# Four product buffers instead of six, delta*x for all channels at once, and an earlier bound for parts on TensorE

## The chip, the cores and the metric

The kernel runs on one core of one Trainium2 chip. The metric is the device time of one execution in microseconds (us). Three timed runs of the kernel before gave 22,543.33, 22,549.62 and 22,551.03 us; the median is 22,549.62 us. The engines are called PE (TensorE, matmul), DVE (VectorE), ACT (ScalarE), POOL (GpSimd) and SP (SyncE, which issues most DMAs).

## The reference

The input is a batch of 8 images of 56 x 56 pixels with 192 channels. Four layers follow one another, each of the form x = x + f(groupnorm(x)): a gated Toeplitz mixer, a shifted-window attention, a depthwise 3 x 3 convolution, and a selective scan in four directions. The change lies in the last. Its core, with 384 inner channels, 16 states and L = 3,136 pixels, is:

```
delta = softplus(delta + delta_bias)
dA    = exp(delta * A)                  # per channel, state, pixel
dBu   = (delta * u) * B                 # u is the convolved input
hs    = scan(a1*a2, a2*b1 + b2)         # h[t] = dA[t]*h[t-1] + dBu[t]
y     = sum over states of hs * C  + D * u
```

The four directions are added up, then come a layer norm over channels, a gate and an output projection.

## The kernel before, in words

Two early stages (the mixer's projections and its Toeplitz products) run alone, up to about 2,340 us, and the front (below) of the first image after them. From 3,735 us on everything is organised around one long loop over the scan.

**Pairs.** The scan's work is cut into chunks of 448 pixels: 8 images (`b`), 4 directions (`slot`) and 7 chunks (`j`), 224 chunks in all. A chunk has 3 blocks of 128 channels (`d`) and 8 groups of two states (`k`). One (chunk, `d`, `k`) is a pair, and a batch is the 672 pairs of one image; there are 5,376 pairs. For pair number `g` the kernel issues:

- `inject` (L990): POOL multiplies du = delta*x by B into `hs` (five buffers);
- `decay` (L1000): ACT computes exp(delta*A) into a PSUM tile `ps_a` (two buffers), two instructions;
- `initial` and `keep_state`: ACT copies the state in and out;
- `scan` (L1010): DVE scans, 898 elements a partition;
- `times_c` (L1019): the product h*C into `hc` (six buffers), on POOL for k in 1, 4, 6 and on DVE for the other five;
- `add_up` (L1032): PE adds the two halves of `hc` into `ps_y`, by two matmuls with the identity.

`times_x` (L979) computes du for one channel block on POOL, from `delta` and a tile `xcd` that `load_xc` (L968) brings in; both have two buffers. `load_xc` also serves the sums of slot 2, through `xds`: it is issued at k = 2 and read at k = 4. `load_bc` brings B and C for the next chunk while the last channel block runs, and `load_delta` brings delta for the next chunk at (d, k) = (1, 0).

**Parts.** Beside the pairs run the parts. `front(b)` holds all other layers of the next image: gate, attention, conv2, inner (input projection and convolution) and steps (delta, B and C of the scan). `finish` holds the norm, the gate and the output projection of eight rows of a finished image. Both are generators; at each `yield` the planner may go on to the next piece. `front` works in one SBUF area (`slab`), so one image's front follows the other. The convolution of inner is issued in thirds of three matmuls (L803) and then evicted by ACT (L812). A front must have stored a chunk's delta before its scan may begin; the loop forces the front at (1, 0) of the chunk before, where that isn't so (L1176).

**The order.** All is written out by hand in one static order for each engine, by the loop at L1168. In iteration `g` it issues, in this order: the du work if it is due, `inject` of g+2, the product of g-1 if it is POOL's, `keep_state` of g-1, `decay` of g+1, `initial` of g+2, `scan` of g, the product of g if it is DVE's, loads, the sums of a finished channel block, then pieces of parts (`parts.step`), and `add_up` of g-2. The planner (`Parts`, L1053) keeps a booked time for P, A, D and E (POOL, ACT, DVE, PE), with costs written in the code: 2.09 us for an inject, 1.1 us on E for an `add_up`, 0.60 us for a matmul of 448 columns. `n1` is the booked begin of the next scan. A piece of a part goes in if its booked ends stay inside the limits of L1221; each refusal adds 3.0 us of grace (L1074). A part that holds a PSUM bank after a piece waits for the next step (L1099).

The program does not take waits from this booking: engines wait for each other by the real dependences and buffers alone.

Of the kernel before, what the change touches and what calls it, by code (L numbers as in the profile page):

```python
# [15 lines left out]
F32 = mybir.dt.float32  # L16
# [11 lines left out]
CH = 448  # L28
# [5 lines left out]
ND = DI // 128  # L34
NG = 2
# [46 lines left out]
def model(ctx: ExitStack, tc: tile.TileContext, a: dict, out: bass.AP):  # L82
# [144 lines left out]
    with (  # L227
# [9 lines left out]
        for ax in range(2):  # L237
# [4 lines left out]
            for c0 in range(D1 // CP):  # L242
# [8 lines left out]
                for c1 in range(0, CP, TC):  # L251
                    t = tm[n_t % 3]
                    n_t += 1
                    e = ext[1 - ax][c0 * CP + c1 : c0 * CP + c1 + TC, :]
# [25 lines left out]
    with (  # L280
# [54 lines left out]
        for i in range(WS):  # L335
            for u in range(2):
                for j in range(WS):
                    at = (i * 2 + u) * WS + j
# [614 lines left out]
        bms, cms, deltas, dus, xcs, states, hss, das, hcs, yps, xds = ({} for _ in range(11))  # L953
# [6 lines left out]
        def load_bc(i, k):  # L960
            b, slot, j = chunks[i]
            for ts, name, r0 in ((bms, "bm", 0), (cms, "cm", NS)):
                ts[i, k] = bcp.tile([128, NG, CH], F32, name=name)
                r = slot % 2 * 32 + r0 + NG * k
                src = bc_d[slot // 2][b][r : r + NG, j * CH : (j + 1) * CH]
                nc.sync.dma_start(out=ts[i, k], in_=src.unsqueeze(0).to_broadcast([128, NG, CH]))

        def load_xc(i, d):  # L968
            b, slot, j = chunks[i]
            t = sp.tile([128, CH], F32, name="xcd", bufs=2)  # L970
            nc.sync.dma_start(out=t, in_=xc_d[slot // 2][b][:, d, j * CH : (j + 1) * CH])
            return t

        def load_delta(i):
            b, slot, j = chunks[i]
            delta = deltas[i] = delta2[:, i % 2]
            nc.sync.dma_start(out=delta[:, :, 1 : CH + 1], in_=dl_d[slot][b][:, :, j * CH : (j + 1) * CH])

        def times_x(i, d):  # L979
            du = dus[i, d] = sp.tile([128, 1, CH], F32, name="du", bufs=2)  # L980
            nc.gpsimd.tensor_mul(du[:, 0, :], deltas[i][:, d, 1 : CH + 1], xcs.pop((i, d)))  # L981

        def tokens(i):

            return (slice(0, CH), CH, 0) if chunks[i][1] % 2 else (slice(1, CH + 1), 0, CH)

        def on_pool(d, k):
            return k in (1, 4, 6)

        def inject(g):  # L990
            i, d, k = pairs[g]
            hs = hss[g] = sp.tile([128, NG, CH + 1], F32, name="hs", bufs=5)
            nc.gpsimd.tensor_mul(hs[:, :, tokens(i)[0]], dus[i, d].to_broadcast([128, NG, CH]), bms[i, k])  # L993

        def initial(g):
            i, d, k = pairs[g]
            src = zero2 if i % NCH == 0 else states[i - 1][:, d, NG * k : NG * k + NG]
            nc.scalar.copy(hss[g][:, :, tokens(i)[1]], src)  # L998

        def decay(g):  # L1000
            i, d, k = pairs[g]
            slot = chunks[i][1]
            dA = psa.tile([128, 1024], F32, name="ps_a")
            dA = das[g] = dA[:, : NG * (CH + 1)].rearrange("p (n t) -> p n t", n=NG)
            at = slot % 2
            for n in range(NG):
                c = NG * k + n
                nc.scalar.activation(  # L1008
                    dA[:, n, :], deltas[i][:, d, at : at + CH + 1], AF.Exp, scale=negA[:, slot, d, c : c + 1]
                )  # L1010
# [8 lines left out]
        def times_c(g):  # L1019
            i, d, k = pairs[g]  # L1020
            h = hss[g] if on_pool(d, k) else das[g]
            hc = hcs[g] = sp.tile([128, NG, CH], F32, name="hc", bufs=6)
            (nc.gpsimd if on_pool(d, k) else nc.vector).tensor_mul(hc, h[:, :, tokens(i)[0]], cms[i, k])  # L1023

        def keep_state(g):
# [27 lines left out]
        class Parts:  # L1053
# [8 lines left out]
            def run(self, engine, cost, *after):  # L1062
                self.t[engine] = max(self.t[engine], 0.0, *after) + cost
                return self.t[engine]
# [72 lines left out]
        with tc.manual_schedule():  # L1137
            for k in range(NP):
                load_bc(0, k)
            load_delta(0)  # L1140
            xcs[0, 0] = load_xc(0, 0)
            times_x(0, 0)
            ahead, last = 2, len(pairs) - 1
            parts = Parts()
            run = parts.run

            fed, set_, scanned, taken, summed = ([0.0] * (len(pairs) + ahead + 8) for _ in range(5))

            def feed(g):
                inject(g)  # L1150
                fed[g] = run("P", 2.09, taken[g - 5] if g > 4 else 0.0)

            def take(g):
                times_c(g)
                after = scanned[g], summed[g - 6] if g > 5 else 0.0
                taken[g] = run("P", 2.0, *after) if on_pool(*pairs[g][1:]) else run("D", 1.09, *after)

            def prepare(g):
                decay(g)
                set_[g] = run("A", 1.3, taken[g - 2] if not on_pool(*pairs[g - 2][1:]) else scanned[g - 2])  # L1160

            for g in range(ahead):
                feed(g)
            initial(0), initial(1)
            prepare(0)
            ahead_of, b_next = None, 1
            ending, anything = None, dict.fromkeys("ADE", 1e9)
            for g, (i, d, k) in enumerate(pairs):  # L1168
                b, slot, j = chunks[i]
                if ahead_of not in parts.clients and b_next < B:  # L1170
                    ahead_of = parts.add(front(b_next), "front")
                    b_next += 1
                more = i + 1 < len(chunks)
                if more and d == 1 and k == 0:
                    b1, slot1, j1 = chunks[i + 1]
                    while (b1, slot1 // 2, j1) not in made:  # L1176
                        parts.step(anything, ahead_of)
                    load_delta(i + 1)
                if k in (0, 3) and (d + 1 < ND or more):
                    at = (i, d + 1) if d + 1 < ND else (i + 1, 0)  # L1180
                    if k == 0:
                        xcs[at] = load_xc(*at)
                    else:
                        times_x(*at)
                        run("P", 1.08)
                pi, pd, pk = pairs[g - 1]
                if g + ahead <= last:
                    feed(g + ahead)
                if g and on_pool(pd, pk):
                    take(g - 1)  # L1190
                if g:
                    keep_state(g - 1)
                    run("A", 0.15, scanned[g - 1])
                if g < last:
                    prepare(g + 1)
                if g + 2 <= last:
                    initial(g + 2)
                    run("A", 0.12, taken[g - 3] if g > 2 else 0.0)
                scan(g)
                scanned[g] = run("D", 2.02, set_[g], fed[g])  # L1200
                if not on_pool(d, k):
                    take(g)
                if g and pd == ND - 1 and pi + 1 < len(chunks):
                    load_bc(pi + 1, pk)
                done = (i, d - 1) if d else (i - 1, ND - 1)
                if k == 2 and g > NP and chunks[done[0]][1] == 2:
                    xds[done] = load_xc(*done)
                if i % (4 * NCH) == 0 and b > 0 and (d, k) == (1, 4):
                    while ending.at < 3:
                        parts.step(anything, ending)  # L1210
                if k == 4 and g > NP:
                    sums(*done)
                pb, pslot, pj = chunks[i - 1]
                if i and pslot == 1 and (d, k) == (0, 5):
                    while ending in parts.clients:
                        parts.step(anything, ending)
                    ending = parts.add(finish(pb, pj), "finish")

                n1 = max(parts.t["D"], fed[g + 1], set_[g + 1])
                n2 = n1 + (2.02 if on_pool(*pairs[min(g + 1, last)][1:]) else 3.11)  # L1220
                parts.step({"A": max(n2, fed[g + 2]) - 0.7, "E": n1 + 8.0, "D": 0.2})  # L1221
                if g >= 2:
                    add_up(g - 2)
                    summed[g - 2] = run("E", 1.1, taken[g - 2])
            if on_pool(d, k):
                times_c(last)
            for g in (last - 1, last):
                add_up(g)
            while parts.clients:
                parts.step(anything)  # L1230
            sums(i, d)
            drain(finish(b, j))
# [101 lines left out]
```

## Time and profile before

| what | value |
|---|---|
| median of 3 runs | 22,549.62 us |
| profiled execution: its own time | 22,537.83 us |
| its span | 22,536.1 us |
| PE busy | 18,327.5 us (81%) |
| DVE busy | 16,594.4 us (74%) |
| POOL busy | 16,169.7 us (72%) |
| ACT busy | 12,468.3 us (55%) |
| first and last scan of the loop | 3,735 us, 22,497 us |
| mean granted TensorE clock | 0.90 |
| DMA over the span | 143 GB/s |

The busy times are of one profiled execution. A busy PE is an upper bound, since matmuls are pipelined and the end of each is modelled: the records of `add_up` have a mean of 593 ns but follow each other every 375 ns where they are back to back. Line numbers (L993 and so on) are those of the kernel before. In the lists of waits, "A <- B" says that the engine and line A stood idle and that B's instruction released it. Of one batch, that of the sixth image's front, the stages lie at 15,808 (gate), 16,323 (attention), 17,099 (conv2), 17,338 (inner) and 17,861 to 18,145 us (steps).

### The profile page before, as it was taken

What the parts mean: (1) busy time and instruction counts of PE and PEld (TensorE: products, weight loads), DVE (VectorE), ACT (ScalarE), POOL (GpSimd) and SP (SyncE); (2) the same over time, 40 slices, a digit from 0 to 9 for tenths busy, and PEclk for the clock granted to TensorE, in tenths of its full rate; (3) what the DMA queues carried; (4) which work ended last, traced back from release to release, by engine and by line L of the source; (5) the groups of instructions that cost most, each with busy time, mean ns of one, the idle gap of its engine ahead of it and who ended that gap; (6) DMA issues with size and microseconds to landing.
All of it is one profiled execution on the core that took longest, in us unless ns stands there. A gap on an engine that the chain in (4) does not pass through costs nothing. (4 is left out here: it accounts for less than half of the span.)

```text
span 22536.1 us, 200417 instructions
## 1 busy us (share of the span) xinstructions
PE 18327.5 (81%) x58660; PEld 9644.0 (43%) x58660; DVE 16594.4 (74%) x13156; ACT 12468.3 (55%) x31864; POOL 16169.7 (72%) x8500
## 2 busy tenths in 40 slices
PE   8866677878888889888887888788978897887666
PEld 4566433434443344434443444344533443343233
DVE  3211113997799868997899779976998789968998
ACT  3311234664757566655766566747675666556555
POOL 0000003897889778887898778977897789878999
PEclk9988777999999989999999989998999999998888
DMA  3478215444554455444644455345544554444443
GB/s 90 106 197 189 73 48 159 139 132 143 187 149 123 136 170 167 126 124 159 195 133 124 151 185 146 123 144 182 158 129 131 174 178 124 131 157 165 130 129 114
DMA packets 2536334, 3220.40 MB, mean 143 GB/s; under 512 B 1045261, under 2 KB 2488687, under 8 KB 2504272
## 3 DMA queue, kind: packets, MB, share of 16 engines
q1 hardware_dynamic: 2515010, 3091.32, 46.3%
q0 software_dynamic: 15520, 116.14, 1.4%
q8 instruction: 465, 7.62, 0.1%
q14 instruction: 635, 5.20, 0.1%
q10 hardware_dynamic: 4704, 0.12, 0.0%
HBM read 2631.56 MB, written 575.48 MB: 142 GB/s over the span
## 5 line engine op out<-in xcount | busy, mean ns | idle before, releaser
L993 POOL TENSOR_TENSOR hs<-du,bm 128x896 f32<-128x896 f32 x5376 | 11132.9, 2111 | 53.7 <-DVE ps_a L1017 35.3
L1038 PE MATMUL ps_y<-hc,ident_sb 128*128 128x448 f32 x21504 | 9850.6, 593 | 717.1 <-POOL hc L1023 624.2
L1017 DVE TENSOR_TENSOR_SCAN ps_a<-ps_a,hs 128x898 f32<-128x898 f32 x3360 | 6800.2, 2024 | 1630.8 <-ACT ps_a L1008 1365.3
L1008 ACT ACTIVATE ps_a<-delta,A_logs_sb 128x449 f32<-128x449 f32 x10752 | 6860.9, 638 | 543.6 <-DVE hs L1017 273.4
L1038 PEld LDWEIGHTS ps_y<-hc,ident_sb 128*128 128x128 f32 x21504 | 4296.7, 208 | 4800.2 <-issue 3550.5
L1023 POOL TENSOR_TENSOR hc<-hs,cm 128x896 f32<-128x896 f32 x2016 | 4086.4, 2027 | 1966.0 <-DVE hs L1017 1236.0
L1017 DVE TENSOR_TENSOR_SCAN hs<-ps_a,hs 128x898 f32<-128x898 f32 x2016 | 4065.2, 2016 | 481.1 <-ACT ps_a L1008 337.5
L1023 DVE TENSOR_TENSOR hc<-ps_a,cm 128x896 f32<-128x896 f32 x3360 | 3668.6, 1092 | 278.0 <-PE ps_y L1038 47.5
L1030 ACT COPY state<-ps_a 128x2 f32<-128x2 f32 x3359 | 527.9, 157 | 3604.9 <-DVE hc L1023 3601.7
L981 POOL TENSOR_TENSOR du<-delta,xcd 128x448 f32<-128x448 f32 x672 | 723.7, 1077 | 1397.5 <-DMA xcd<-xc 1384.5
L263 PE MATMUL ps_tz<-tzx,tm 112*112 112x112 f32 x4608 | 889.2, 369 | 466.0 <-issue 298.0
L803 PE MATMUL ps_f<-slab 128*128 128x448 f32 x2646 | 1105.1, 554 | 102.0 <-DMA slab<-dg_d 78.7
L277 POOL DMA_DIRECT2D o<-tzx x192 | 98.0, 514 | 1493.2 <-DVE tzx L269 1017.3
L263 PEld LDWEIGHTS ps_tz<-tzx,tm 112*112 112x112 f32 x4608 | 883.7, 199 | 471.8 <-issue 470.6
L269 DVE COPY tzx<-ps_tz 112x448 f32<-112x448 f32 x288 | 180.0, 625 | 1174.6 <-PE ps_tz L263 800.9
L76 PE MATMUL ps_f<-slab 96*96 96x448 f32 (+6 forms) x2306 | 746.1, 519 | 88.9 <-DMA slab<-x 37.2
L633 PE MATMUL ps_f<-ident_sb,slab 98*98 98x98 f32 x1344 | 334.6, 316 | 594.6 <-ACT slab L626 594.6
L269 ACT COPY tzx<-ps_tz 112x448 f32<-112x448 f32 x288 | 153.3, 532 | 1200.5 <-PE ps_tz L263 982.3
L998 ACT COPY hs<-state 128x2 f32<-128x2 f32 x4608 | 817.4, 177 | 0.0
L803 PEld LDWEIGHTS ps_f<-slab 128*128 128x128 f32 x2646 | 512.9, 195 | 603.3 <-issue 533.3
L735 PE MATMUL ps_f<-slab 96*96 96x448 f32 x1764 | 732.4, 551 | 41.7 <-DVE slab L722 41.2
L618 ACT ACTIVATE slab<-slab,mxs 98x98 f32<-98x98 f32 x1344 | 489.4, 365 | 359.7 <-DVE mxs L615 359.7
(215 smaller groups left out, 17601.5 us busy)
## 6 DMA issues: line engine op xcount, KB each, us to landing
bm<-bc SPq DMA_DIRECT2D x1792, 448.0 KB
cm<-bc SPq DMA_DIRECT2D x1792, 448.0 KB
xcd<-xc SPq DMA_DIRECT2D x840, 224.0 KB
dl<-slab SPq DMA_DIRECT2D x224, 672.0 KB
delta<-dl SPq DMA_DIRECT2D x224, 672.0 KB
tzx<-qv SPq DMA_DIRECT2D x192, 588.0 KB
o<-tzx POOLq DMA_DIRECT2D x192, 588.0 KB, 16.7
slab<-x SPq DMA_DIRECT2D x224, 336.0 KB
```

Source lines behind the costliest of these rows:

```text
L76: return f(*args, **kw)
L263: nc.tensor.matmul(po[:, c, :], t[:, c2 + c, :], x[:, :, c1 + c2 + c], start=True, stop=True)
L735: nc.tensor.matmul(p[:CP, :CH], dg[:, k, t, :], xp[:, u, k, dy : dy + 8, dx : dx + W], start=t == 0, stop=t == 8,)
L803: nc.tensor.matmul(p[:, :CH], dg[:, t, :], xp[:, 8 * j + dy : 8 * j + dy + 8, dx : dx + W], start=t == 0, stop=t == 8,)
L981: nc.gpsimd.tensor_mul(du[:, 0, :], deltas[i][:, d, 1 : CH + 1], xcs.pop((i, d)))
L993: nc.gpsimd.tensor_mul(hs[:, :, tokens(i)[0]], dus[i, d].to_broadcast([128, NG, CH]), bms[i, k])
L998: nc.scalar.copy(hss[g][:, :, tokens(i)[1]], src)
L1008: nc.scalar.activation(dA[:, n, :], deltas[i][:, d, at : at + CH + 1], AF.Exp, scale=negA[:, slot, d, c : c + 1])
L1017: nc.vector.tensor_tensor_scan(h, dA, hs, 0.0, ALU.mult, ALU.add)
L1023: (nc.gpsimd if on_pool(d, k) else nc.vector).tensor_mul(hc, h[:, :, tokens(i)[0]], cms[i, k])
L1030: nc.scalar.copy(states[i][:, d, NG * k : NG * k + NG], h[:, :, tokens(i)[2]])
L1038: nc.tensor.matmul(yps[i, d][:, :CH], ident, hcs[g][:, n, :], start=k + n == 0, stop=k + n == NP + NG - 2)
```

## The change

Three edits go together.

1. `hc` has four buffers instead of six. The planner's `take` books a product behind the sum of pair g-4 instead of g-6.
2. `xcd` and `du` have four buffers instead of two. The three `load_xc` of the next chunk are issued together, at (d, k) = (1, 0) right behind `load_delta`, and the three `times_x` of the next chunk at (1, 6), (1, 7) and (2, 0). Before, each was loaded at k = 0 and multiplied at k = 3 of the channel block before. The first chunk gets all three ahead of the loop.
3. A part's booked end on E has to lie at most 5.0 us behind `n1`, instead of 8.0 us.

The buffers given and taken have the same size in sum: two `hc` of 3,584 bytes a partition, against two `xcd` and two `du` of 1,792 bytes each.

```diff
         def load_xc(i, d):
-            t = sp.tile([128, CH], F32, name="xcd", bufs=2)
+            t = sp.tile([128, CH], F32, name="xcd", bufs=4)
...
         def times_x(i, d):
-            du = dus[i, d] = sp.tile([128, 1, CH], F32, name="du", bufs=2)
+            du = dus[i, d] = sp.tile([128, 1, CH], F32, name="du", bufs=4)
...
         def times_c(g):
-            hc = hcs[g] = sp.tile([128, NG, CH], F32, name="hc", bufs=6)
+            hc = hcs[g] = sp.tile([128, NG, CH], F32, name="hc", bufs=4)
...
             load_delta(0)
-            xcs[0, 0] = load_xc(0, 0)
-            times_x(0, 0)
+            for d in range(ND):
+                xcs[0, d] = load_xc(0, d)
+                times_x(0, d)
...
             def take(g):
                 times_c(g)
-                after = scanned[g], summed[g - 6] if g > 5 else 0.0
+                after = scanned[g], summed[g - 4] if g > 3 else 0.0
...
                     load_delta(i + 1)
-                if k in (0, 3) and (d + 1 < ND or more):
-                    at = (i, d + 1) if d + 1 < ND else (i + 1, 0)
-                    if k == 0:
-                        xcs[at] = load_xc(*at)
-                    else:
-                        times_x(*at)
-                        run("P", 1.08)
+                    for e in range(ND):
+                        xcs[i + 1, e] = load_xc(i + 1, e)
+                if more and (d, k) in ((1, 6), (1, 7), (2, 0)):
+                    times_x(i + 1, d + k - 7 if d == 1 else 2)
+                    run("P", 1.08)
...
-                parts.step({"A": max(n2, fed[g + 2]) - 0.7, "E": n1 + 8.0, "D": 0.2})
+                parts.step({"A": max(n2, fed[g + 2]) - 0.7, "E": n1 + 5.0, "D": 0.2})
```

## The prediction

> **What bounds the kernel now.** I read the groups of instructions first, for what one pair costs each engine; then busy time by stage; then the waits of the worst stage. From the groups (busy time, mean ns | idle ahead of them):
>
> ```profile
> L993 POOL TENSOR_TENSOR hs<-du,bm 128x896 f32<-128x896 f32 x5376 | 11132.9, 2111 | 53.7 <-DVE ps_a L1017 35.3
> L1038 PE MATMUL ps_y<-hc,ident_sb 128*128 128x448 f32 x21504 | 9850.6, 593 | 717.1 <-POOL hc L1023 624.2
> L1023 POOL TENSOR_TENSOR hc<-hs,cm 128x896 f32<-128x896 f32 x2016 | 4086.4, 2027 | 1966.0 <-DVE hs L1017 1236.0
> L1023 DVE TENSOR_TENSOR hc<-ps_a,cm 128x896 f32<-128x896 f32 x3360 | 3668.6, 1092 | 278.0 <-PE ps_y L1038 47.5
> L981 POOL TENSOR_TENSOR du<-delta,xcd 128x448 f32<-128x448 f32 x672 | 723.7, 1077 | 1397.5 <-DMA xcd<-xc 1384.5
> ```
>
> Per pair POOL needs 2.09 (its usual duration) + 3/8 x 2.03 + 1/8 x 1.08 = 2.99 us, DVE 2.02 + 5/8 x 1.09 + about 0.1 = 2.8 us. The loop's 5,376 scans run from 3,735 to 22,497 us, 3.49 us a pair; the last batch, with no front beside it, takes 3.0. So 0.5 us a pair comes from the parts. Three stretches (attention, inner, last batch; columns as in the head line):
>
> ```profile
> core 0: us, PE busy (x) PEld busy (x) DVE busy (x) ACT busy (x) POOL busy (x), PEclk, DMA share, GB/s
> 16323.00:17031.00 708.00, 565.19 (x2027) 276.29 (x2028) 672.68 (x565) 499.09 (x1574) 660.59 (x339) 0.93 0.40 123
> 17338.00:17805.00 467.00, 413.40 (x1099) 213.45 (x1100) 330.00 (x218) 247.35 (x576) 360.89 (x188) 0.93 0.47 150
> 20600.00:22000.00 1400.00, 949.72 (x1937) 423.25 (x1936) 1320.60 (x848) 738.67 (x1936) 1400.00 (x727) 0.86 0.40 128
> ```
>
> The last stretch is POOL's, 100%. Attention runs DVE and POOL at 95% and 93%, 3.15 us a pair. In inner they fall to 71% and 77% and a pair takes 3.9 to 4.5 us: TensorE binds there. Four records of a sum take 1.5 us at their spacing of 0.375 us, a convolution third of six takes 2.25, together 3.75 us. The waits from 17,350 to 17,800 us (total, times, longest):
>
> ```profile
> ACT slab L812 <- PE ps_f L803: 103.1, 18, 9.5
> ...
> DVE ps_a L1017 <- ACT ps_a L1008: 64.3, 28, 5.3
> POOL hc L1023 <- DVE hs L1017: 45.7, 14, 7.9
> ...
> DVE hs L1017 <- ACT ps_a L1008: 20.8, 9, 4.6
> ```
>
> ACT stands at the eviction of a convolution, the decays behind it are late, then DVE, then POOL. One such moment in order of time:
>
> ```profile
> 17526.39 1.09 DVE L1023 TENSOR_TENSOR hc<-ps_a,cm 128x896 f32<-128x896 f32 x1 [0.73 <-PE ps_y L1038]
> ...
> 17528.65 0.63 ACT L812 ACTIVATE slab<-ps_f,cb_sb 128x448 f32<-128x448 f32 x1 [7.64 <-PE ps_f L803]
> ...
> 17533.88 2.02 DVE L1017 TENSOR_TENSOR_SCAN hs<-ps_a,hs 128x898 f32<-128x898 f32 x1
> ...
> 17536.04 2.08 POOL L1023 TENSOR_TENSOR hc<-hs,cm 128x896 f32<-128x896 f32 x1 [7.50 <-DVE hs L1017]
> ```
>
> The first line is a product waiting 0.73 us for a buffer although there are six.
>
> **What the Trainium skill says.** "TensorE: Matmul & The Clock Gate", Architectural detail: ACT and DVE are strict FIFO, and matmuls keep program order. The lines above agree: decays stand 7.64 us behind one eviction. "FP8 and Floating Point Precision", TensorE Precision Notes: true FP32 takes four passes; here each 448-column matmul of the source is two records, 0.75 us together, while the planner books 0.55 to 0.60. "Perfetto Trace Analysis", Optimization Strategy: a gap that repeats can mean too few buffers for the next tile; with six, products waited for sums 190.7 us (47.5 on DVE, 143.2 on POOL). "SBUF — State Buffer", SBUF: two separate sides: the DVE/GpSimd port lock needs a DVE operation with two SBUF inputs. Scan and product on DVE have one input in PSUM, so moving du should start no new contention; inject's usual 2.09 us is the same in both middle stages.
>
> **The change, part by part.**
>
> *hc from six to four.* A product of pair g now needs the sum of g-4 finished. Behind a waiting DVE product stand the next scan, then ACT's decay of g+2 (two ps_a buffers); behind a POOL product stand inject and the finish part's multiplies L915 and L922; SP's reload of cm waits too. I laid every product's start in the trace against the end of the sum four pairs back: 641 DVE products would have waited 1,557 us and 193 POOL products 442 us, nearly all in the stages of conv2 to steps. That 1,999 us is the upper bound. If instead the idle time that DVE has ahead of its scans swallows the shift, because that idle already follows TensorE, 20 us is left, 17 of it in the last batch, where POOL has no slack. The lower bound for buffers alone is 0. What isn't swallowed: where a waiting POOL product stands directly ahead of L915 or L922, TensorE gets its next matmul later; 45 of 220 such multiplies, by 79 us in sum. I take 20 + 79 = +99.
>
> *The limit from 8 to 5 us.* It stops a part whose modelled end on E is too far out. But a part that holds a PSUM bank advances once per step anyway: in TensorE's order only 21 to 27 of a batch's 672 pairs hold more than one part between two sums. A third books 1.8 us and a sum 1.1, 2.9 against the planner's pair of 2.97, so its E stays near n1 + 2 to n1 + 4. A refused part gets 3.0 us of grace, which is the old limit one pair later. I take 0; bounds are rivals C and D. The shorter dependence in take only moves booked times.
>
> *du and xcd.* All that moves: three loads issued with delta at (d 1, k 0), three POOL multiplies at (1,6), (1,7), (2,0) instead of at k 3. The counts stay 672 multiplies and 672 loads, plus the 168 for the sums. On SP one burst of four issues (0.4 to 0.7 us each) passes ahead of the product loads of the next chunk, which start eight pairs later; parts' loads behind it lose under 2 us. xcd's four slots suffice: a reused slot was always read pairs before. On POOL, (1,6) to (2,0) holds 3 x 2.09 + 2.03 + 3 x 1.08 = 11.5 us, against 9 for three pairs at 3.0. POOL's lead of about two pairs covers that 2.5 us; uncovered it is 0.5 us net of POOL's other slack on 224 chunks, 112 us. I take 0. The load now leads by six pairs instead of three. POOL's waits for xcd are 1,384.5 us with one of 1,270.9 before the loop, so 113.6 can be won, 0 at least. They lie in steps, where POOL has slack, so I take a third: -38. At the start two more loads and multiplies precede the first inject: 2 x 1.08 + 0.9, +3.
>
> The sum: the profiled execution took 22,537.8 us (span 22,536.1). 22,538 + 99 + 0 - 38 + 3 = 22,602. The runs' median is 12 us above the profiled one: 22,614, forecast 22,615 us, +0.3%. About 0.2% (45 us) is what a measurement tells from no change.
>
> **The rivals.**
>
> A is the forecast: buffers cost a little more than the earlier loads give, 22,595 to 22,800.
>
> B, nothing to be seen, 22,505 to 22,595: TensorE binds inner and POOL the rest, and a wait for hc only renames a wait for ACT. For it: the 20 us left after absorption, and that the limit hardly bites. It is also the case that the change doesn't do what it says. Against: the 79 us behind POOL. Price: 22,550.
>
> C, faster: the backlog on TensorE shrinks, evictions come earlier. Scans waited 85 us for decays in 450 us of inner; TensorE's own idle in that stage is 467 - 413 = 54 us. Half of it, 27 us in 7 batches, is -189: 22,360. It decides if a good part of the 35 convolution tiles a batch is delivered earlier to ACT. Against: the few pairs with two parts.
>
> D, much slower: the front runs past its batch. It takes a batch of pairs now; its first step is stored 54 pairs before the batch begins and needed 16 before, so 38 pairs of slack. If each of 35 convolution tiles loses a pair, the slack goes in the second batch; then 35 parts x 2.25 us are forced with scans standing, 79 us a batch, less 35 x 0.9 us saved by pairs of 3.0 instead of 3.9: +47 in five batches, 236, on top of A: 22,850. From a loss of about 10 pairs a batch on it is visible.
>
> **How the numbers follow.** A 0.45, B 0.25, C 0.18, D 0.12. Faster 0.18 (C), same 0.25 (B), slower 0.57 (A and D). The range 22,440 to 22,830 leaves out the far half of C and of D and the bound of 1,999 us, which would need that no idle absorbs anything; A alone is 22,595 to 22,800.
>
> **What would show it.** Products' waits for ps_y rise from 191 us to 600 to 1,000, mostly in inner and steps; waits of L812 for L803 and of scans for ACT fall there; TensorE's order stays one part per pair; POOL's waits for xcd in the loop fall below 30 us; pairs of attention stay at 3.15 us and the last batch at 3.0. I am wrong if attention or the last batch slows (grouped du or hc then bind POOL), if the front ends at other pairs (C or D), or if inner's pairs go below 3.9.

## The result, and the profile after

| | kernel before | changed kernel |
|---|---|---|
| median | 22,543.33 us (19 runs, 22,509.14 to 22,570.23) | 22,507.13 us (19 runs, 22,491.45 to 22,536.51) |
| profiled execution: its own time | 22,537.83 us | 22,523.93 us |
| its span | 22,536.1 us | 22,522.1 us |

The ratio of the two kernels' runs is 0.9989 (95% interval 0.9982 to 0.9996), 0.11% less; the medians differ by 36 us. That lies within the 0.2% called no change, and on the other side of it than the forecast of +0.3%. The forecast was wrong, and a near zero is no sign that the edits are idle: the experiments below find terms of -0.57% and +0.38% in it. The median falls just inside rival B's range (22,505 to 22,595), but by terms that cancel and not for B's reasons; that is luck. The two profiled executions differ by 14 us only, so their stages show less of the gain than the medians do.

Two groups of instructions of the changed kernel:

```profile
L1023 DVE TENSOR_TENSOR hc<-ps_a,cm 128x896 f32<-128x896 f32 x3360 | 3667.7, 1092 | 1207.7 <-PE ps_y L1038 921.5
...
L981 POOL TENSOR_TENSOR du<-delta,xcd 128x448 f32<-128x448 f32 x672 | 719.6, 1071 | 1268.7 <-DMA xcd<-xc 1268.7
```

Counts and durations are those of before. What moved is the idle time: ahead of DVE's products it rises from 278.0 to 1,207.7 us, with the sum of an earlier pair as its releaser, and ahead of du it falls from 1,397.5 to 1,268.7 us, of which one wait before the loop is left. The waits over the whole span say where the rise was paid from. Of the kernel before:

```profile
DVE ps_a L1017 <- ACT ps_a L1008: 1365.3, 500, 349.9
...
ACT slab L812 <- PE ps_f L803: 742.9, 135, 14.2
...
DVE hs L1017 <- ACT ps_a L1008: 337.5, 188, 8.0
...
ACT ps_a L1008 <- DVE hs L1017: 273.4, 230, 1.8
...
PE ps_f L927 <- POOL slab_f L922: 217.5, 43, 10.8
...
POOL hc L1023 <- PE ps_y L1038: 143.2, 77, 6.0
```

Of the changed kernel:

```profile
engine line waited for: us in total, times, longest us
DVE hc L1023 <- PE ps_y L1038: 921.5, 571, 14.3
DVE ps_a L1017 <- ACT ps_a L1008: 895.4, 302, 349.9
...
POOL hc L1023 <- PE ps_y L1038: 570.6, 237, 8.9
...
ACT slab L812 <- PE ps_f L803: 506.1, 139, 5.4
...
DVE hs L1017 <- ACT ps_a L1008: 253.6, 110, 9.8
...
ACT ps_a L1008 <- DVE hs L1017: 72.9, 69, 1.8
```

Before, products waited 47.5 + 143.2 = 191 us for sums; now it is 921.5 + 570.6 = 1,492. Scans waited 1,365.3 + 337.5 = 1,703 us for decays; now 895.4 + 253.6 = 1,149. Evictions of the convolution waited 742.9, now 506.1. About 1,300 us more of waiting for buffers made no time in the sum. Most of it stands where DVE and POOL stood before, for another reason. One more wait fell, that of decays for a scan (from 273.4 to 72.9 us); what it is comes with the experiments.

Busy time by stage of the changed kernel (inner of the sixth image's front, and a stretch of the last batch; columns as in the prediction):

```profile
17404.00:17882.00 478.00, 429.35 (x1183) 227.83 (x1184) 342.60 (x230) 267.37 (x617) 380.13 (x197) 0.95 0.48 152
20700.00:22000.00 1300.00, 874.66 (x1791) 386.35 (x1790) 1221.37 (x787) 688.15 (x1800) 1298.07 (x673) 0.87 0.39 126
```

The limits of the stages are the same: inner has TensorE at 90%, the last batch POOL at 100%. To compare whole loops, I counted in each trace the scans begun in each stage of the seven fronts, and took from the stage's time 3.0 us for each of them, the price of a pair in the last batch. What is left is the excess, the time that the parts cost. A stage begins with a first matmul (L470 for gate, L658, L735, L803 and L852 for the others), so the head of a front, which loads and projects before L470, is counted under "no front", and some ten pairs ahead of the first gate in no column:

| | loop, us | gate | attention | conv2 | inner | steps | no front |
|---|---|---|---|---|---|---|---|
| before: pairs | | 1,079 | 1,701 | 448 | 892 | 517 | 729 |
| before: excess, us | 18,763 | 369 | 341 | 329 | 997 | 493 | 102 |
| after: pairs | | 1,072 | 1,701 | 447 | 900 | 568 | 677 |
| after: excess, us | 18,748 | 343 | 369 | 316 | 992 | 497 | 97 |

A pair of inner costs 4.10 us (4.12 before), one of steps 3.87 (3.95). Steps takes 51 pairs more, and pairs counted under "no front" fall from 729 to 677. They are mostly the last batch behind the end of the last front, which comes 16 pairs into that batch before and 63 after. The front is later: its steps stage begins 58 pairs ahead of its batch in the last front before, and 16 after.

### The profile page after: what moved, and what is told of

It is laid out like the page before. It is cut to its first block, busy times and chain, and to the rows that moved or that the text cites. A ratio compares the mean times of both kernels' runs of the same rounds, so it can differ in the third digit from the quotient of the medians.

```text
span 22522.1 us, 201129 instructions
## 1 busy us (share of the span) xinstructions
PE 18316.9 (81%) x58660; PEld 9648.2 (43%) x58660; DVE 16557.5 (74%) x13156; ACT 12501.5 (56%) x31864; POOL 16170.0 (72%) x8500
## 5 line engine op out<-in xcount | busy, mean ns | idle before, releaser
L1038 PE MATMUL ps_y<-hc,ident_sb 128*128 128x448 f32 x21504 | 9845.4, 592 | 742.9 <-POOL hc L1023 665.7
L1017 DVE TENSOR_TENSOR_SCAN ps_a<-ps_a,hs 128x898 f32<-128x898 f32 x3360 | 6796.3, 2023 | 1093.1 <-ACT ps_a L1008 895.4
L1008 ACT ACTIVATE ps_a<-delta,A_logs_sb 128x449 f32<-128x449 f32 x10752 | 6859.9, 638 | 355.0 <-DVE hs L1017 72.9
L1023 DVE TENSOR_TENSOR hc<-ps_a,cm 128x896 f32<-128x896 f32 x3360 | 3667.7, 1092 | 1207.7 <-PE ps_y L1038 921.5
L1017 DVE TENSOR_TENSOR_SCAN hs<-ps_a,hs 128x898 f32<-128x898 f32 x2016 | 4063.4, 2016 | 331.2 <-ACT ps_a L1008 253.6
L981 POOL TENSOR_TENSOR du<-delta,xcd 128x448 f32<-128x448 f32 x672 | 719.6, 1071 | 1268.7 <-DMA xcd<-xc 1268.7
L803 PE MATMUL ps_f<-slab 128*128 128x448 f32 x2646 | 1090.3, 548 | 60.1 <-DMA slab<-dg_d 48.0
L735 PE MATMUL ps_f<-slab 96*96 96x448 f32 x1764 | 725.5, 547 | 40.8 <-DVE slab L722 40.8
L803 PEld LDWEIGHTS ps_f<-slab 128*128 128x128 f32 x2646 | 507.7, 193 | 560.7 <-issue 502.5
L1030 ACT COPY state<-hs 128x2 f32<-128x2 f32 x2016 | 379.0, 188 | 581.5 <-DVE hs L1017 545.1
```

What stands on the lines that cost most here:

```text
L735: nc.tensor.matmul(p[:CP, :CH], dg[:, k, t, :], xp[:, u, k, dy : dy + 8, dx : dx + W], start=t == 0, stop=t == 8,)
L803: nc.tensor.matmul(p[:, :CH], dg[:, t, :], xp[:, 8 * j + dy : 8 * j + dy + 8, dx : dx + W], start=t == 0, stop=t == 8,)
L1008: nc.scalar.activation(dA[:, n, :], deltas[i][:, d, at : at + CH + 1], AF.Exp, scale=negA[:, slot, d, c : c + 1])
L1017: nc.vector.tensor_tensor_scan(h, dA, hs, 0.0, ALU.mult, ALU.add)
L1030: nc.scalar.copy(states[i][:, d, NG * k : NG * k + NG], h[:, :, tokens(i)[2]])
L1038: nc.tensor.matmul(yps[i, d][:, :CH], ident, hcs[g][:, n, :], start=k + n == 0, stop=k + n == NP + NG - 2)
```

## The experiments

Four sets of runs, each on one chip with its own runs of the kernel before, whose medians were 22,554.66, 22,532.33, 22,529.19 and 22,549.59 us. Within a set I compare medians, between sets ratios to the kernel before (with 95% intervals; they rest on all runs and can differ a little from the quotient of the medians).

### The parts alone (first set)

The buffers alone, with no other edit; the order of the instructions stays that of before on every engine.

```diff
-            hc = hcs[g] = sp.tile([128, NG, CH], F32, name="hc", bufs=6)
+            hc = hcs[g] = sp.tile([128, NG, CH], F32, name="hc", bufs=4)
```

> The kernel before with four hc buffers and nothing else: the planner still books a product behind the sum of six pairs back, so every engine's order stays that of before and only the waits differ. My forecast's theory (a POOL product that waits for a sum holds up the finish part's multiplies): +20 to +99 us, ratio 1.001 to 1.0045. Rival, the wait only takes the place of a wait for ACT: ratio within 0.999 to 1.001, products' waits for sums up from 191 us to over 900 us, scans' waits for ACT down by about as much. If the buffers themselves gave the gain: 0.9985.

22,541.45 us, 0.9995 (0.9987 to 1.0003): no difference. The waits of this kernel over the whole span:

```profile
DVE hc L1023 <- PE ps_y L1038: 993.0, 608, 13.6
DVE ps_a L1017 <- ACT ps_a L1008: 954.6, 338, 349.8
...
POOL hc L1023 <- PE ps_y L1038: 541.5, 220, 11.2
ACT slab L812 <- PE ps_f L803: 428.7, 115, 7.0
...
DVE hs L1017 <- ACT ps_a L1008: 231.0, 94, 5.5
...
PE ps_f L927 <- POOL slab_f L922: 204.1, 42, 11.0
...
ACT ps_a L1008 <- DVE hs L1017: 81.5, 84, 1.8
```

Products wait 1,535 us instead of 191, and the loop takes 18,765 us against 18,763. Scans wait 517 us less for decays, evictions 314 us less. The output projection's matmuls (L927), which were to be late behind waiting POOL products, wait 204.1 us against 217.5. In the sum the longer waits for buffers cost nothing. The zero is a net one, though: the waits of decays for a scan fall from 273.4 to 81.5 us, and these aren't waits for a buffer that the kernel's text asks for (see below, four buffers and the bound). So how much the two missing buffers cost by themselves isn't shown.

The buffers, with the new place of the du work. To keep the planner's order, the 1.08 us were left booked at k = 3, and only the multiplies moved.

```diff
-            t = sp.tile([128, CH], F32, name="xcd", bufs=2)
+            t = sp.tile([128, CH], F32, name="xcd", bufs=4)
...
-            du = dus[i, d] = sp.tile([128, 1, CH], F32, name="du", bufs=2)
+            du = dus[i, d] = sp.tile([128, 1, CH], F32, name="du", bufs=4)
...
-            hc = hcs[g] = sp.tile([128, NG, CH], F32, name="hc", bufs=6)
+            hc = hcs[g] = sp.tile([128, NG, CH], F32, name="hc", bufs=4)
...
-                if k in (0, 3) and (d + 1 < ND or more):
...
+                    for e in range(ND):
+                        xcs[i + 1, e] = load_xc(i + 1, e)
+                if k == 3 and (d + 1 < ND or more):
+                    run("P", 1.08)
+                if more and (d, k) in ((1, 6), (1, 7), (2, 0)):
+                    times_x(i + 1, d + k - 7 if d == 1 else 2)
```

> Four hc buffers, and delta*x loaded and multiplied at the new places with four buffers; the planner's bookings are left where they were, so PE, DVE and ACT keep the order of before. Against the run with four hc buffers alone this is the du edit by itself. My forecast's term: -38 us (-0.17%). Upper bound: -114 us, all of POOL's waits for xcd. Rival, POOL has slack where those waits lie: 0 to -15 us. If the three multiplies in a row bind POOL: +50 us or more, in attention.

22,597.48 us, 1.0017 (1.001 to 1.0024), 56 us above the buffers alone. The move costs time. Its profiled execution took 22,566.91 us, 26 us more than that of the buffers alone, so the trace holds about half of the loss. One place in order of time, POOL and DVE; the last column is what the instruction stood idle for:

```profile
8169.17 1.14 POOL L981 TENSOR_TENSOR du<-delta,xcd 128x448 f32<-128x448 f32 x1
...
8174.33 0.99 POOL L981 TENSOR_TENSOR du<-delta,xcd 128x448 f32<-128x448 f32 x1
...
8175.27 6.19 POOL L993 TENSOR_TENSOR hs<-du,bm 128x896 f32<-128x896 f32 x3
...
8177.39 2.04 DVE L1017 TENSOR_TENSOR_SCAN ps_a<-ps_a,hs 128x898 f32<-128x898 f32 x1 [1.60 <-POOL hs L993]
```

The same place with the multiplies where they were (buffers alone):

```profile
8188.04 6.17 POOL L993 TENSOR_TENSOR hs<-du,bm 128x896 f32<-128x896 f32 x3
...
8191.44 2.02 DVE L1017 TENSOR_TENSOR_SCAN ps_a<-ps_a,hs 128x898 f32<-128x898 f32 x1
```

POOL is behind a finish part here in both. With the multiplies in its queue, the scan at (2, 2) stands 1.60 us for its inject; without them the inject is done by 8190.12 and the scan, at 8191.44, doesn't wait for it. Over the loop, that scan waits 62 us for its inject against 13, and the time from the inject's end to the scan's begin has a median of 2.7 us (4.6) and 0.03 in the lowest tenth (0.8). Other scans wait some 29 us less for their injects, so that 20 us of these waits are left over the whole loop.

The bound alone, with six buffers:

```diff
-                parts.step({"A": max(n2, fed[g + 2]) - 0.7, "E": n1 + 8.0, "D": 0.2})
+                parts.step({"A": max(n2, fed[g + 2]) - 0.7, "E": n1 + 5.0, "D": 0.2})
```

> The kernel before with the bound on parts' booked TensorE end at 5.0 us instead of 8.0, six hc buffers, old du. My forecast: the bound hardly bites, 0 us, ratio 0.999 to 1.001, and PE's stages keep their length in pairs. Rival, the order is what gave the gain: ratio 0.997 to 0.9985, with ACT's waits at the convolution's eviction (before: 743 us) down to about 500 us as in the changed kernel. Rival, it hurts and the buffers or du make up for it: over 1.001.

22,538.22 us, 0.9995 (0.9987 to 1.0003). No difference in the sum, but not for lack of an effect: steps takes 579 pairs (517), and 673 are counted without a front (729). The front falls so far behind that the loop forces it from the fifth on: the scans stand three times, for 32 to 34 us. Decays wait 369.4 us for a scan, where they waited 273.4. Excess falls in conv2, steps and the pairs without a front by 76 us, and rises in gate, attention and inner by 72.

The buffers with the planner's new booking:

```diff
-            hc = hcs[g] = sp.tile([128, NG, CH], F32, name="hc", bufs=6)
+            hc = hcs[g] = sp.tile([128, NG, CH], F32, name="hc", bufs=4)
...
-                after = scanned[g], summed[g - 6] if g > 5 else 0.0
+                after = scanned[g], summed[g - 4] if g > 3 else 0.0
```

> Four hc buffers and the planner told of it (a product booked behind the sum four pairs back); bound 8.0 and du as before. If four buffers need the tighter bound, this is the slow one: 1.002 to 1.006, with parts booked at up to 8 us and products waiting over 1,500 us. If the booking is what gave the gain: 0.998. If neither matters: 0.999 to 1.001.

22,610.14 us, 1.0022 (1.0013 to 1.0031): the booking alone costs 0.27%, 69 us. It does change the order. Later booked products move `n1` out, the limits that hang on `n1` let parts in sooner, and the front runs faster: 845 pairs for inner (888), 774 pairs without a front (730). Against the buffers alone, excess rises by 72 us in gate, 22 in attention and 21 where no front is; inner gives 63 back.

The du work alone, with six product buffers, was not measured.

### The parts together, and taken out of the changed kernel (second set)

The changed kernel with the old bound:

```diff
-                parts.step({"A": max(n2, fed[g + 2]) - 0.7, "E": n1 + 5.0, "D": 0.2})
+                parts.step({"A": max(n2, fed[g + 2]) - 0.7, "E": n1 + 8.0, "D": 0.2})
```

> The changed kernel with the old bound of 8.0 us on parts' TensorE end. If the bound is what the other two edits need: about the time of four buffers with the booking alone, ratio 1.002 to 1.004. If the bound does nothing, as forecast: 0.999, the changed kernel's time.

22,637.47 us, 1.0046 (1.0034 to 1.0059). So the bound is worth 0.57% in the changed kernel (0.9989 against 1.0046), some 128 us.

The changed kernel with the old du work:

```diff
-            t = sp.tile([128, CH], F32, name="xcd", bufs=4)
+            t = sp.tile([128, CH], F32, name="xcd", bufs=2)
...
-            du = dus[i, d] = sp.tile([128, 1, CH], F32, name="du", bufs=4)
+            du = dus[i, d] = sp.tile([128, 1, CH], F32, name="du", bufs=2)
...
-                    for e in range(ND):
-                        xcs[i + 1, e] = load_xc(i + 1, e)
-                if more and (d, k) in ((1, 6), (1, 7), (2, 0)):
...
+                if k in (0, 3) and (d + 1 < ND or more):
+                    at = (i, d + 1) if d + 1 < ND else (i + 1, 0)
```

> The changed kernel with delta*x loaded and multiplied as before (two buffers each). With PE, DVE and ACT in a frozen order the du edit cost 0.22% (1.0017 against 0.9995). If that cost is the edit's own, this kernel is faster than the changed one: 0.997. If the planner's order made up for it, or the cost belongs to that one order: 0.999. If du is the part that gains: 1.001 or more, with POOL waiting some 110 us for xcd again.

22,423.83 us, 0.9951 (0.9937 to 0.9964). Without its du edit the changed kernel would be 0.5% faster than before; the edit costs 0.38% (0.9989 against 0.9951), some 86 us. Its last front begins steps 16 pairs ahead of its batch, as in the changed kernel.

The changed kernel with the old booking:

```diff
-                after = scanned[g], summed[g - 4] if g > 3 else 0.0
+                after = scanned[g], summed[g - 6] if g > 5 else 0.0
```

> The changed kernel with four hc buffers but the planner still booking a product behind the sum six pairs back. If telling the planner costs (four buffers told were 1.0022, untold 0.9995): faster than the changed kernel, 0.997. If booking only shifts the order, which can go either way: between 0.998 and 1.002.

22,510.49 us, 0.999 (0.9984 to 0.9997), as the changed kernel: with the bound at 5.0 the booking makes no difference here. With the old booking the loop forces the last two fronts, though: the scans stand for 44 and 43 us, and in the changed kernel they never do.

Four buffers and the bound, nothing else; the order is that of the bound alone, on all engines:

```diff
-            hc = hcs[g] = sp.tile([128, NG, CH], F32, name="hc", bufs=6)
+            hc = hcs[g] = sp.tile([128, NG, CH], F32, name="hc", bufs=4)
...
-                parts.step({"A": max(n2, fed[g + 2]) - 0.7, "E": n1 + 8.0, "D": 0.2})
+                parts.step({"A": max(n2, fed[g + 2]) - 0.7, "E": n1 + 5.0, "D": 0.2})
```

> Four hc buffers and the bound of 5.0 us, old booking, old du. If effects add: 0.9995 for the buffers times 0.9995 for the bound, 0.999. If the order is a lottery of about 0.2%: anything from 0.998 to 1.002, and not to be told from the single edits.

22,462.83 us, 0.9967 (0.9955 to 0.998). Against the bound with six buffers (0.9995) the same instructions in the same order end 0.28% earlier with two buffers less, and the intervals don't meet. Against four buffers with the old bound (0.9995) it is again 0.28%. The two edits that are worth nothing alone are worth 0.33% together, 70 us between the medians; neither range named ahead had that.

Products wait 1,252 us for sums. Between six and four buffers at this bound, excess falls in gate from 392 to 338 us, in attention from 379 to 363, in steps from 460 to 442, and rises by 21 in conv2. In gate the traces show what went: a wait of decays. Over the whole span, with six buffers and this bound, then with four:

```profile
ACT ps_a L1008 <- DVE hs L1017: 369.4, 268, 1.8
```

```profile
ACT ps_a L1008 <- DVE hs L1017: 82.1, 73, 1.8
```

One of them in gate, first with six buffers (DVE's product and scan, then ACT's decay):

```profile
6274.41 1.09 DVE L1023 TENSOR_TENSOR hc<-ps_a,cm 128x896 f32<-128x896 f32 x1
6275.42 2.02 DVE L1017 TENSOR_TENSOR_SCAN hs<-ps_a,hs 128x898 f32<-128x898 f32 x1
...
6277.47 1.31 ACT L1008 ACTIVATE ps_a<-delta,A_logs_sb 128x449 f32<-128x449 f32 x2 [1.77 <-DVE hs L1017]
```

The same instructions with four:

```profile
6273.67 1.09 DVE L1023 TENSOR_TENSOR hc<-ps_a,cm 128x896 f32<-128x896 f32 x1
6274.68 2.02 DVE L1017 TENSOR_TENSOR_SCAN hs<-ps_a,hs 128x898 f32<-128x898 f32 x1
...
6274.99 1.31 ACT L1008 ACTIVATE ps_a<-delta,A_logs_sb 128x449 f32<-128x449 f32 x2
```

This decay, of pair g+1, takes the buffer of `ps_a` that the product in the first line has just read. The scan in the second line is that of pair g, on the other buffer, and the kernel's text makes no decay wait for it. With six buffers the decay starts when that scan has ended, with four right behind the product. So the order is the same, but the two programs don't hold the same waits: with six buffers 481 decays wait for a semaphore of DVE, with four 237 (462 and 243 at the old bound). Engines do wait for more here than the real dependences and buffers. In gate 62 decays start late by this, 103 us in sum, and none with four buffers. At the scans right behind the 62, the six-buffer kernel falls back by 75 us; in the rest of gate it regains 20. That makes up the 54 us of gate. At the old bound the same wait is gone too (87 us in gate, then none), and gate falls by 40 us, but conv2 and attention give it back. Why the number of buffers of `hc` changes these waits is not in the traces.

A second thing changes with them, and may follow from them: the records of L470, gate's matmuls with the identity, take 276 ns with six buffers and 268 with four (274 and 268 at the old bound), with a mean granted clock of 0.94 and 0.97 where they start.

### Where the du work hurts (third set)

The kernel with du moved and the order frozen, but the multiplies spread:

```diff
-                if more and (d, k) in ((1, 6), (1, 7), (2, 0)):
-                    times_x(i + 1, d + k - 7 if d == 1 else 2)
+                if more and (d, k) in ((1, 4), (1, 6), (2, 1)):
+                    times_x(i + 1, (k - 4) // 2 if d == 1 else 2)
```

> Four hc buffers, the loads of xcd grouped as in the change, the frozen order of PE, DVE and ACT, but the three multiplies at (1,4), (1,6) and (2,1), where POOL has no product in the same iteration. Theory: three multiplies in a row use up POOL's lead, and the scan at (2,2) waits for its inject (62 us over the loop, 13 with the old places). Then this kernel is at 0.9995 or a little below, and that wait under 25 us. Rival, the grouped loads cost (SP's burst): it stays at 1.0017.

22,536.57 us, 1.0006 (0.9997 to 1.0014), against 1.0017 grouped and 0.9995 with the old places: the same 672 multiplies, two and three pairs apart, win back about half of the loss (the intervals of 1.0006 and 1.0017 just overlap). The lead ahead of the scan at (2, 2) is back at 4.6 us in the median, and that scan waits 14 us for its inject; but scans at (2, 0), which had waited 3 us, now wait 17. Neither forecast is met in full.

The changed kernel with the three loads early and in one group, but the multiplies at their old places (with five `xcd` buffers, two `du`):

```diff
-            t = sp.tile([128, CH], F32, name="xcd", bufs=2)
+            t = sp.tile([128, CH], F32, name="xcd", bufs=5)
...
+                    for e in range(ND):
+                        xcs[i + 1, e] = load_xc(i + 1, e)
+                if k == 3 and (d + 1 < ND or more):
+                    times_x(*((i, d + 1) if d + 1 < ND else (i + 1, 0)))
+                    run("P", 1.08)
```

> Four hc buffers, booked, bound 5.0, multiplies at the old places at k 3, only the three loads grouped at (1,0) with five xcd buffers. Against the same kernel with old loads (0.9951). My forecast's term for the earlier load: -38 us, 0.9934, with POOL's waits for xcd in the loop gone (137 us there). Rival, POOL has slack where it waits for xcd: 0.9951 within 0.0007.

22,405.2 us, 0.995 (0.9938 to 0.9963), against 0.9951 with the late loads. POOL's waits for `xcd` were 1,404.7 us with the late loads, 1,267.2 of it in one wait before the loop; now that one wait, 1,270.7, is all there is. PE, DVE, ACT and POOL keep their order exactly. So 137 us in the loop become none, and the time doesn't move: the early loads bring nothing, and the loss comes from the multiplies' place (in the changed kernel their bookings move with them).

### The size of the bound (third and fourth set)

With the old du work (the changed kernel without its du edit), bounds of 4.0 and 6.5:

```diff
-                parts.step({"A": max(n2, fed[g + 2]) - 0.7, "E": n1 + 5.0, "D": 0.2})
+                parts.step({"A": max(n2, fed[g + 2]) - 0.7, "E": n1 + 4.0, "D": 0.2})
```

> The kernel of four hc buffers, booked, old du, with the bound at 4.0 us instead of 5.0. Theory: the tighter the bound, the fewer pairs hold two parts where front and finish overlap, so that stage takes more pairs (517 at 8.0, about 576 at 5.0) at less time each; at 4.0 the front reaches its last possible place earlier and is then forced: 0.994 to 0.998. If 5.0 is only one draw of a lottery of orders: anything from 0.993 to 1.002.

```diff
-                parts.step({"A": max(n2, fed[g + 2]) - 0.7, "E": n1 + 5.0, "D": 0.2})
+                parts.step({"A": max(n2, fed[g + 2]) - 0.7, "E": n1 + 6.5, "D": 0.2})
```

> The same with the bound at 6.5 us. Theory of the bound: between the run at 8.0 with the booking (1.0022) and the one at 5.0 (0.9951), 0.997 to 1.000, with a pair count of the steps stage between theirs. Lottery: anything from 0.993 to 1.002, with no order among 4.0, 5.0, 6.5 and 8.0.

With the loads early, bounds of 5.5 and 4.6:

```diff
-                parts.step({"A": max(n2, fed[g + 2]) - 0.7, "E": n1 + 5.0, "D": 0.2})
+                parts.step({"A": max(n2, fed[g + 2]) - 0.7, "E": n1 + 5.5, "D": 0.2})
```

> Loads grouped, multiplies at the old places, four hc buffers, booked; bound 5.5 us. If the bound of 5.0 works by spreading front and finish over more pairs, a neighbour does so too: 0.994 to 0.998. If 5.0 was one lucky order: 1.000 to 1.002, as at 6.5 and 4.0.

```diff
-                parts.step({"A": max(n2, fed[g + 2]) - 0.7, "E": n1 + 5.0, "D": 0.2})
+                parts.step({"A": max(n2, fed[g + 2]) - 0.7, "E": n1 + 4.6, "D": 0.2})
```

> The same with the bound at 4.6 us. Theory: still spread, but the front reaches its last possible place a batch or two earlier, and from there on it is forced with scans standing: 0.996 to 0.999, with late batches of 2,420 us. Lottery: 1.000 to 1.002 with no such late batches.

The six bounds side by side (all with four buffers, the new booking and the du multiplies at their old places):

| bound, us | ratio | median, us | pairs without a front | steps' start, pairs ahead of the batch, fronts 1 to 7 |
|---|---|---|---|---|
| 8.0 (booked, first set) | 1.0022 (1.0013 to 1.0031) | 22,610.14 | 774 | 80, 83, 94, 97, 97, 97, 97 |
| 6.5 | 1.0007 (1.0001 to 1.0014) | 22,544.95 | 699 | 73, 69, 66, 59, 49, 46, 42 |
| 5.5 (loads early) | 0.9924 (0.991 to 0.9938) | 22,382.98 | 681 | 73, 59, 52, 49, 35, 27, 22 |
| 5.0 (loads early) | 0.995 (0.9938 to 0.9963) | 22,405.2 | 672 | 73, 60, 51, 47, 33, 24, 16 |
| 4.6 (loads early) | 0.996 (0.9948 to 0.9973) | 22,458.58 | 671 | 71, 56, 44, 32, 20, 15, 15 |
| 4.0 | 1.0008 (1.0 to 1.0016) | 22,541.85 | 674 | 63, 51, 36, 15, 15, 15, 15 |

Of the ranges named ahead, 4.6 falls into its own, 5.5 does better than its own, and 4.0 and 6.5 miss that of the theory, which had both below 1.000 or at it.

About 15 pairs ahead is as late as it can be; then the loop forces the front. At 4.0 the fourth front is there, with one stop of the scans of 26 us, and from the fifth on they stand twice in each front, some 90 us together. The timeline of that kernel at the end of the fifth front's inner, DVE's scan, with what it stood idle for:

```profile
15567.87 2.03 DVE L1017 TENSOR_TENSOR_SCAN hs<-ps_a,hs 128x898 f32<-128x898 f32 x1 [55.62 <-ACT ps_a L1008]
```

TensorE's in the same place:

```profile
15508.35 6.93 PE L803 MATMUL ps_f<-slab 128*128 128x448 f32 x18
15547.50 4.82 PE L852 MATMUL ps_f<-slab 128*128 128x448 f32 x6 [32.22 <-DMA slab<-xc]
```

The scans stand for 56 us. In it the last convolution is evicted, run through Silu, stored and read again for steps: TensorE waits 32.22 us for that DMA. Batches of the loop take 2,352 to 2,378 us in this kernel until then, and 2,440, 2,424 and 2,423 afterwards. At 4.6 two stops, of 44 and 45 us, are left; at 5.0 and 5.5 there is none. The fastest bounds are those where the front comes near its last possible place and isn't forced. 6.5, which isn't forced either, gains nothing, and the runs don't say why.

A last run asks whether 5.0 had a lucky order: the margin on ACT is changed, which gives another order in places (4% of TensorE's records stand elsewhere).

```diff
-                parts.step({"A": max(n2, fed[g + 2]) - 0.7, "E": n1 + 5.0, "D": 0.2})
+                parts.step({"A": max(n2, fed[g + 2]) - 0.65, "E": n1 + 5.0, "D": 0.2})
```

> The same at 5.0 us, and only ACT's margin in the planner at 0.65 us instead of 0.7, to get another order at the same bound. Theory: 0.993 to 0.997. Lottery: 0.998 to 1.002.

22,428.64 us, 0.9947 (0.9934 to 0.9959), against 0.995. Another order, if a near one, gives the same gain. The kernel at 5.5 is the best that was found, faster than both kernels of this case: 22,382.98 us.

## Why the prediction was wrong

**"hc from six to four" (+99).** It measured -13 us in the first set, no difference. The step that failed is the 79 us: "where a waiting POOL product stands directly ahead of L915 or L922, TensorE gets its next matmul later". L927 waited no longer (204.1 us against 217.5). That DVE's idle time swallows the shift fits the waits: 1,344 us more of product waits stand against 831 us less of waits for decays and convolutions. But a term that the forecast didn't have is in the zero, the 192 us of decays waiting for a scan that went with the two buffers; so the measured zero doesn't say what the product waits cost. In the changed kernel the product waits went past the forecast of 600 to 1,000 us, to 1,492, and this made no time in the sum. Rival B's mechanism, "a wait for hc only renames a wait for ACT", fits that in the main, and is not proven by it. The Trainium skill ("Perfetto Trace Analysis", Optimization Strategy) reads a gap that repeats on the engine that should be saturated as a possible lack of buffers; here 608 such gaps on DVE came with two buffers less, and the time stayed (0.9995).

**"The limit from 8 to 5 us" (0).** This is the main error, and it has the sign. With four buffers the bound is worth -0.28%, in the changed kernel -0.57%. The step that failed is "its E stays near n1 + 2 to n1 + 4", argued from the few pairs with two parts: that there was nothing to refuse. The count was right and stayed: by the planner's cost per matmul, 157 pairs hold more than 1.9 us of parts before, and 165 after. Yet the bound bites: it doesn't thin the full pairs, it holds the whole front back, so that the last one begins steps 16 pairs ahead of its batch instead of 58 (some 97 in the changed kernel at the old bound). This is rival D's motion, "the front loses pairs", but not D's saving of 0.9 us a pair. Against the changed kernel at the old bound 95 pairs leave the last column (772 to 677), 86 us by that price; but the three columns between which pairs move (inner, steps, no front) save only 7 us of the 123 between the two profiled loops. The other 116 lie in gate (65), conv2 (39) and attention (12), which keep their pairs. Part of gate's share is to be seen: at the old bound the front is so early that 124 pairs of gate stand beside a finish part, at 86 us of excess, and at 5.0 none does. With four buffers and the old booking the three columns save 35 us of 67, and conv2 42. So where the bound's gain lies is shown, and the cause stays open in the main. D's other half, the forced front, comes at 4.0 and 4.6, and with the old booking at 5.0 too; in the changed kernel the slack of the seven fronts just lasts. C, which had the right sign, was right in its result only: a pair of inner takes 4.10 us as before.

**"The shorter dependence in take only moves booked times."** It measured +0.27% with the old bound (69 us), -0.16% at 5.0 with the old du work (0.9951 against 0.9967, 39 us between the medians of one set, though the intervals overlap), nothing in the changed kernel. Booked times are what the limits are measured by, so the order moves with them. At 5.0 the old booking forces three fronts (98 us of standing scans), the new one none.

**"du and xcd" (-38).** It measured +56 us in a frozen order and about +86 in the changed kernel (0.9951 to 0.9989). The step that failed is "POOL's lead of about two pairs covers that 2.5 us". The lead is about that in the median (6.7 us over all scans of the kernel before) but not where it is needed: at (2, 2) it is 5.4 us in the median and already 0.03 in the lowest tenth. Behind a finish part it is gone, and there the multiplies make the scan late. The uncovered bound, 112 us, was named and not chosen. The -38 failed too: 137 us of waits for loads vanished for nothing (0.995 against 0.9951). All of them lay where POOL had slack, not two thirds. Waits for `xcd` in the loop did fall to none, as said.

**Attention and the last batch.** A pair of attention takes 3.18 us in the sixth image's front (3.15 forecast). The last batch takes 2,045 us, 3.04 a pair, against 2,018, a little slower than said. Without the new du it takes 2,034, so some 11 of the 27 us go with du, on a POOL that is at 100% there. The other 16 go with the last front, which now reaches 63 pairs into the batch instead of 16: with the bound alone it reaches 64 and the batch takes 2,042.

**The sum** of what was measured, in two orders of taking the edits one behind the other. Buffers -0.05%, booking +0.27, du +0.24 (1.0022 to 1.0046), bound -0.57: together -0.11%. Buffers -0.05%, bound -0.28, booking -0.16, du +0.38: together -0.11%. Both must end there, since each step is the difference of two measured kernels. The terms aren't independent; the bound is worth most where the booking has hurried the front, and du costs most where the rest is fast.

What stays open: why two buffers of `hc` less take waits from the decays; what makes gate and conv2 cheaper when the front is later; why 6.5 loses (its steps stage has 556 us of excess in 567 pairs, 461 in 576 at 5.0); how much of one bound's value is its particular order, since 5.5 and 5.0 differ by 0.26% with nearly the same slack.

## What to carry to other kernels

A wait for a buffer is a cost only if something else doesn't stand at the same place: test by the number of buffers alone, in the same order, before it is priced, and then compare all waits of the two traces, since the programs may differ in more than that one. A static planner's limit sets how far ahead background work runs: ask which stages then fall beside other work, and how far the slack lasts until work is forced. Work that is grouped on an engine near its limit must be covered by the least lead that it has there, not by the mean; spread it, or leave it.

## What the runs showed of the hardware

Three things were not expected. Two programs with the same instructions in the same order on every engine differed by 0.28%. Their waits differ by more than the two buffers ask for: 62 decays of gate start late in one, by 103 us in sum, and none in the other. That this makes gate's part of the difference is shown by the lag at those places; the rest of the difference isn't traced. The mean granted TensorE clock at the matmuls of L470 was 0.94 in one and 0.97 in the other, and their records lasted 276 and 268 ns. And a forced change from inner to steps kept TensorE idle for 32.22 us, from its last convolution until that had been evicted, run through Silu, stored and read back: about the time of ten pairs, where nothing covers it.
